# A GNN layer on one core: lead-in of the plan with longer transfers, bias parts from one row, message products by block, earlier due times

## The chip, the cores and the metric

The kernel runs on one core of a Trainium2 chip. The core has five engines that work side by side, each through its own queue in order: PE (TensorE, matmuls), DVE (VectorE), ACT (ScalarE), POOL (GpSimd) and SP (SyncE, which here only issues transfers). They wait for one another through semaphores. The metric is device time in microseconds; less is better. The time before is 669.11 us, the median of three runs.

## The reference

A graph with 6250 nodes of 128 features and 100,000 edges, sorted by their target. Each edge carries the source's features through one of two weight matrices, by the edge's type, and the messages are summed at the target. A third matrix is applied to the node itself; then come relu, the residual and a layer norm.

```
Xs = X[src]
m_data = Xs @ W_data.T + b_data
m_ctrl = Xs @ W_control.T + b_control
msg = jnp.where((edge_types == 0)[:, None], m_data, m_ctrl)
agg = jax.ops.segment_sum(msg, dst, num_segments=X.shape[0])
out = relu(agg + (X @ W_self.T + b_self))
x = _layernorm(x + out, axis=-1)
```

## The kernel before

**Messages.** There are 49 blocks of 128 nodes. For each block PE multiplies the node features (f32, from `xc`) with both message matrices in `w_sb` (L448) and adds the bias by a second matmul of a 0/1 matrix `one3` with `brows` (L450), whose first three rows hold the bias split into three bf16 parts that add up to the f32 value. Two blocks share a PSUM bank `g` of a ring of three. The sum is split into three bf16 parts as well and kept in SBUF as `m3`: for the first ten pairs (DQ) by ACT copies and DVE subtractions (L459 to L465, buffer `r1`), for the others by copies and matmuls with minus the identity (`minus`, L473). Each pair also goes to a table in memory (L479).

**Ranks.** Nodes are taken in 35 windows of 160 targets, in groups of 1, 2, and eight times 4 windows (GROUPS). For a group, `ranks` loads the windows' edges (`win`, 2688 edges each, 21 columns of 128), and for each of the 21 columns k it builds one-hot rows `hots` (L645, DVE), adds them up in the bank `rk` by matmuls with `tri` and `rest` (L655, PE) and takes the maximum (L659, DVE): the slot of each edge among the edges of its target window and source block. One column's reduce must be done before PE adds the next, so the 21 columns are a chain; `rk` and the `hots` exist once, so the groups follow one another as well. A packed map of slots is scattered (L674 to L689), written to memory (`packed`) and read back broadcast to all partitions as `rows`. Edges that found no slot are put in a list (L726 to L790, a row of short instructions), gathered from the table (`sr`) and joined as `gl`.

**Sums.** For each window and each of 25 quadruples of source blocks, stage 1 (L867) picks messages out of `m3` by `rows` into a `g` bank, ACT or DVE copies them to `gs` (L413 or L414), and stage 2 (L881, L884) adds them to the window's sums `a` by one-hot `hot` (L854). `close` then does relu, residual and layer norm. The last 650 nodes are summed another way: their edges' messages are gathered from the table tile by tile (`t_msg`, L931, L942).

**Where the edges of a window are** is found at the start: `r0` loads the target of every 200th edge (L257), DVE and PE count which lie below each window's first node, `er` gathers one row of 200 edges for each window (L353), and from it comes `first`, the first edge of each window (L375). Only group 0, which begins at edge 0, needs no `first`.

**What sets the order.** No engine's order is written out by hand. Each piece of work is given to a planner with its engine, an assumed length, a due time, what it reads and writes, and `lat`, the time from its end until its result can be used elsewhere. `Plan.run` then walks through a simulated time: on the engine that is free soonest it takes, among the work that is ready at that moment, that with the smallest due time. The program is issued in that order, and each engine keeps it on the chip, whatever the real lengths are. SP's transfers are assumed to take 0.1 us of the queue. Buffers of one name form a ring in the order of their first due time. Due times in the lead-in are:

- message products of pair q: 4 + 1.3 q
- ranks of group gi, column k: when + 2 + step k; the one-hot row 2 us sooner; the list at when + 6.5 + 21 step
- window w: from T0 + 13 w on, and the tiles of the last nodes from T0 + 2.5 x 13 on

**Lines that the prediction follows.** L257 `r0` load, L263 `b3` load, L335 to L351 counting, L353 `er`, L361 to L366 its use, L399 to L408 the bias parts on DVE, L439 `xc`, L448/L450 products, L502, L508, L511, L925 loads that `close` and the last nodes need (issued by SP at the start, as they wait for nothing), L606 to L659 ranks.

Of the kernel before, what the change touches and what calls it, by code (L numbers as in the profile page):

```python
# [23 lines left out]
D3 = 3 * D  # L24
# [206 lines left out]
def sums_over_windows(ctx, tc, x, xt, edges, w, bias, out, total):  # L231
# [16 lines left out]
    def C(shape, dtype, name):  # L248
        return Buf(plan, const, shape, dtype, name, 1)

    T0 = 46.0
    TW = 13.0
# [5 lines left out]
        r0.t, edges.rearrange("(p h k) c -> p h (k c)", p=125, h=RH)[:, :, 1:2]), 0.0, w=[r0],  # L258
        lat=2.0)
    w_sb = C([D, D3], F32, "w_sb")  # L260
    b3 = C([3, D3], F32, "b3")
    add("ACT", 0.1, lambda: A.dma_start(w_sb.t, w), 0.0, [], [w_sb], lat=2.5)
    add("ACT", 0.1, lambda: A.dma_start(b3.t, bias.to_broadcast([3, D3])), 0.0, [], [b3], lat=2.5)  # L263

# [77 lines left out]
    def count_rows():  # L342
# [13 lines left out]
        in_offset=bass.IndirectOffsetOnAxis(ap=row_i.t[:, 0:1], axis=0)),  # L356
        0.5, [row_i], [er], lat=2.5)
    dst_f = C([NBD, RL], F32, "dst_f")
# [19 lines left out]
    def load_edges(b, n, out_, due, buf, key, engine):  # L378
        def fn():
# [6 lines left out]
            else:  # L386
# [4 lines left out]

    part = C([3, D3], BF16, "part")
    left = C([3, D3], F32, "left")
    acc3 = C([3, D3], F32, "acc3")
    part2 = C([3, D3], BF16, "part2")
    brows = C([P, D3], BF16, "brows")
    bd = 2.0
    vec(1, D3, lambda: V.memset(brows.t, 0.0), [], [brows], 0.3)
    vec(bd, D3, lambda: V.tensor_copy(part.t, b3.t), [b3], [part])  # L399
    vec(bd, D3, lambda: V.tensor_scalar_mul(acc3.t, part.t, ident.t[:3, 0:1]),  # L400
        [part, ident], [acc3])
    vec(bd, D3, lambda: V.tensor_sub(left.t, b3.t, part.t), [b3, part], [left])
    vec(bd, D3, lambda: V.tensor_copy(part2.t, left.t), [left], [part2])
    vec(bd, D3, lambda: V.scalar_tensor_tensor(acc3.t, part2.t, ident.t[:3, 1:2], acc3.t,
                                               op0=ALU.mult, op1=ALU.add),
        [part2, ident, acc3], [acc3])
    vec(bd, D3, lambda: V.tensor_sub(left.t, left.t, part2.t), [part2, left], [left])
    vec(bd, D3, lambda: V.scalar_tensor_tensor(brows.t[:3, :], left.t, ident.t[:3, 2:3], acc3.t,  # L408
                                               op0=ALU.mult, op1=ALU.add),
        [left, ident, acc3], [brows])  # L410

# [18 lines left out]
    for q in range(NS):  # L430
# [12 lines left out]

        def products(bs=bs, c=c, xa=xa, mp=mp, q=q):
            for i, b in enumerate(bs):
                o = mp.t[:, 256 * i : 256 * i + 256]
                at = (b - c * CH) * P
                T.matmul(o, xa.t[:, at : at + P], w_sb.t[:, : 2 * D], start=i == 0, stop=False,  # L448
                         skip_group_check=True)
                T.matmul(o, one3.t, brows.t[:, : 2 * D], start=False, stop=q < DQ,  # L450
                         skip_group_check=True)
        add("PE", 0.55 * nb, products, due, [xa, w_sb, one3, brows], [mp])
        ts = slice(4 * q, 4 * q + 2 * nb)
# [499 lines left out]
    for gi, nw in enumerate(GROUPS):  # L953
        if gi == 0:
            when, step, engines = 4.0, 0.5, ["SP"]
        elif gi == 1:
            when, step, engines = 19.0, 0.9, ["SP", "ACT"]
        else:
            when, step, engines = T0 + w0 * TW - 58, 1.8, ["SP"]
            if gi == 2:  # L960
                when, step = 40.0, 1.3
        todo.append((gi, w0, nw, when, step, engines))
        w0 += nw
# [8 lines left out]
    total_tiles = sum(GT)  # L972
    g0, g1 = T0 + 2.5 * TW, T0 + (NW - 2.5) * TW
    done = 0
# [151 lines left out]
```

## Time and profile before

| | before |
|---|---|
| median of the runs | 669.11 us (669.08 to 672.03) |
| the profiled execution, its own time | 620.9 us |
| its span | 619.1 us |
| PE busy | 540.9 us (87%), 13418 matmuls |
| DVE busy | 521.1 us (84%) |
| ACT busy | 445.7 us (72%) |
| POOL busy | 115.1 us (19%) |
| mean granted TensorE clock | 0.982 |

The durations below come from that one profiled execution, whose time is 48.2 us less than the median of the timed runs. In a line of the timeline stand the start and length in microseconds, the engine, the line of the kernel, the operation, what it writes and reads, its shape, how often; and in brackets how long the engine stood idle just before and what ended that. A q behind an engine's name is its queue issuing a transfer. Names such as `brows` or `rk` are the program's own, with the numbers of buffers left out (so `one3` is "one", `b3` is "b").

### The profile page before, as it was taken

How to read it: one execution, taken by the hardware profiler on the slowest of the kernel's cores; microseconds unless marked ns; L12 is line 12 of the kernel's file. 1: busy time of each engine (PE TensorE's matmuls, PEld its weight loads, DVE VectorE, ACT ScalarE, POOL GpSimd, SP SyncE). 2: the span in 40 equal slices, each digit the busy share in tenths (PEclk: the TensorE clock that was granted, in tenths of full speed). 3: DMA queues.
4: the chain of work that ended last, by engine and by line, in shares of the span. 5: the costliest groups of instructions: out<-in, count | busy, mean ns of one | idle time of the engine just before them, and what ended most of it. 6: DMA issues, size and time to landing. Idle time of an engine off the chain costs nothing.

```text
span 619.1 us, 31669 instructions
## 1 busy us (share of the span) xinstructions
PE 540.9 (87%) x13418; PEld 415.5 (67%) x13418; DVE 521.1 (84%) x1846; ACT 445.7 (72%) x1153; POOL 115.1 (19%) x119
## 2 busy tenths in 40 slices
PE   3899959979998898989979998998899889998991
PEld 2555637757776677767767877777777678776670
DVE  4899789989999899988998999899988987866602
ACT  1477736757677767867867788778777777788991
POOL 1000230020421034310134410045100333110000
PEclk9999988989999999999999999999999999999997
DMA  4688651063135223540344143315420443043001
GB/s 113 194 269 266 196 178 38 25 207 104 44 103 153 84 65 100 177 127 5 118 141 140 51 134 99 101 50 168 133 85 4 156 122 109 24 139 105 27 4 28
DMA packets 58893, 67.85 MB, mean 110 GB/s; under 512 B 19707, under 2 KB 49906, under 8 KB 58743
## 3 DMA queue, kind: packets, MB, share of 16 engines
q1 hardware_dynamic: 45585, 48.25, 24.3%
q0 software_dynamic: 5664, 10.97, 6.7%
q10 hardware_dynamic: 7494, 6.53, 3.4%
q8 instruction: 107, 1.75, 1.1%
q14 instruction: 43, 0.35, 0.2%
HBM read 50.72 MB, written 13.27 MB: 103 GB/s over the span
## 4 chain that ended last, share of the span: by engine, by line
DVE 55%; PE 30%; ACT 5%; DMA 4%; issue 4%; SPq 1%; POOL 0%; ACTq 0%; DVEq 0%
DVE hot L854 10%; DVE slot L659 9%; PE a L881 9%; PE g L867 8%; DVE hots L645 4%; PE rk L655 4%; DVE rows L847 4%; DVE two L680 4%; ACT gs L413 3%; PE g L448 3%; DVE s L530 3%; DVE st L542 2%; DVE hr L674 2%; DVE xr L538 2%; PE a L884 2%
## 5 line engine op out<-in xcount | busy, mean ns | idle before, releaser
L413 ACT CAST gs<-g 128x384 bf16<-128x384 f32 x836 | 353.8, 481 | 93.5 <-PE g L867 88.6
L867 PE MATMUL g<-m,rows 128*32 128x384 bf16 x3430 | 316.8, 329 | 1.9 <-issue 1.1
L881 PE MATMUL a<-gs,hot 128*32 128x384 bf16 x3360 | 306.0, 331 | 9.1 <-ACT gs L413 5.1
L867 PEld LDWEIGHTS <-rows 128*32 128x32 bf16 x3430 | 217.4, 135 | 14.6 <-issue 2.1
L884 PE MATMUL a<-gs,hot 128*32 128x128 bf16 x2520 | 200.9, 220 | 0.1
L881 PEld LDWEIGHTS <-hot 128*32 128x32 bf16 x3500 | 153.4, 95 | 62.8 <-issue 27.0
L931 POOL DMA_INDIRECT t_msg<-table,t_idx x93 | 95.5, 1027 | 243.3 <-PE ga L942 196.9
L659 DVE TENSOR_REDUCE slot<-rk 128x4 f32<-128x392 f32 (+2 forms) x210 | 106.6, 507 | 18.2 <-PE rk L655 15.5
L854 DVE TENSOR_TENSOR hot<-iota_b,to_d 128x800 bf16<-128x800 bf16 x175 | 93.6, 565 | 21.0 <-PE a L884 16.6
L884 PEld LDWEIGHTS <-hot 128*32 128x32 bf16 x2625 | 98.0, 96 | 4.7 <-issue 0.3
L655 PE MATMUL rk<-hots,rest 128*32 128x392 bf16 (+2 forms) x800 | 73.2, 317 | 25.9 <-DVE slot L659 25.2
L655 PE MATMUL rk<-hots,tri 128*32 128x392 bf16 (+2 forms) x840 | 82.7, 314 | 0.0
L655 PEld LDWEIGHTS <-rest 128*32 128x32 bf16 x800 | 34.9, 96 | 48.4 <-issue 43.6
L645 DVE TENSOR_TENSOR hots<-iota_b,st 128x392 bf16<-128x392 bf16 (+2 forms) x210 | 60.1, 327 | 1.8 <-PE vt L689 1.6
L797 POOL DMA_INDIRECT sr<-table,at x18 | 17.1, 949 | 183.4 <-DVE at L785 99.9
L847 DVE TENSOR_SCALAR rows<-rows,pid 128x1568 bf16<-128x1568 bf16 x70 | 43.0, 635 | 0.0
L942 PE MATMUL ga<-t_msg,t_hot 128*32 128x384 bf16 x363 | 39.0, 326 | 2.7 <-DVE s L530 2.2
L655 PEld LDWEIGHTS <-tri 128*32 128x32 bf16 x840 | 36.3, 97 | 3.5 <-issue 0.3
L530 DVE TENSOR_TENSOR s<-s,a 128x128 f32<-128x128 f32 x70 | 19.8, 284 | 18.0 <-ACT s L527 16.8
L448 PE MATMUL g<-w_sb,xc 128*128 128x256 f32 x98 | 32.8, 430 | 1.3 <-PE rk L655 0.9
L689 PEld LDWEIGHTS <-two 128*64 128x64 bf16 x735 | 18.6, 108 | 16.7 <-DVE two L680 13.7
L689 PE MATMUL vt<-hots,two 128*64 128x98 bf16 x735 | 24.1, 208 | 6.0 <-DVE two L680 5.7
(174 smaller groups left out, 568.7 us busy)
## 6 DMA issues: line engine op xcount, KB each, us to landing
rows<-packed SPq DMA_DIRECT2D x35, 784.0 KB
table<-m SPq DMA_DIRECT2D x12, 384.0 KB
table<-m ACTq DMA_DIRECT2D x12, 384.0 KB
xc<-in_xt SPq DMA_DIRECT2D x8, 320.0 KB
xr<-in_x SPq DMA_DIRECT2D x8, 256.0 KB
out<-xr SPq DMA_DIRECT2D x8, 256.0 KB
gl<-sr SPq DMA_DIRECT2D x35, 48.0 KB
xc<-in_xt ACTq DMA_DIRECT2D x6, 256.0 KB
```

What stands on the lines that cost most here:

```text
L413: [("ACT", act(cols), lambda: A.copy(o(), src())), ("DVE", dve(cols), lambda: V.tensor_copy(o(), src()))], None, None, due, r, w, lat)
L448: T.matmul(o, xa.t[:, at : at + P], w_sb.t[:, : 2 * D], start=i == 0, stop=False, skip_group_check=True)
L645: vec(due - (2.0 if k else 0.5), nw * NT, lambda k=k, hot=hot, k0=k0: V.tensor_tensor(hot.t[:, k - k0].rearrange("p w (c d) -> p w c d", d=2),
L655: T.matmul(acc.t[R * j : R * j + R, : nw * NT], wt.t[:, R * j : R * j + R], m, start=start, stop=stop, skip_group_check=True)
L659: vec(due, nw * NT, lambda k=k: V.tensor_reduce(slot.t[:, k, :], acc.t[:, : nw * NT].rearrange("p (w c) -> p w c", c=NT), axis=AX.X, op=AL ...
L689: T.matmul(vv()[q : q + 64, i // 2, :], two.t[:, (k - k0) * nw + i].rearrange("p f r -> p (f r)"), hot.t[:, k - k0, i, :], start=k == 0 an ...
L847: add("DVE", dve(half * NT, 0.26), lambda sp=sp, rs=rs: V.tensor_scalar(sp.t[:, rs], sp.t[:, rs], pid1.t, None, op0=ALU.is_equal), due - 4 ...
L854: V.tensor_tensor(hot2.t[:, c0 : c0 + 5].rearrange("p g (c d) -> p g c d", d=2), iota1_b.t.rearrange("p (c d) -> p c d", d=2)[:, None].to_ ...
L867: T.matmul(gp.t[R * t : R * t + R, :D3], sp.t[:, :, 4 * g + t], m3.t[:, 4 * g + t, :], start=True, stop=True)
L881: T.matmul(a.t[R * j : R * j + R, :D3], hot2.t[:, g, R * j : R * j + R], gs.t, start=g == 0, stop=False, skip_group_check=True)
L884: T.matmul(a.t[R * c : R * c + R, D3:], hot2.t[:, g, P:], gs.t[:, c * D : (c + 1) * D], start=False, stop=last, skip_group_check=True)
L931: add("POOL", 1.25, lambda m=m, k=k: G.indirect_dma_start(out=m.t, out_offset=None, in_=table[:, :], in_offset=bass.IndirectOffsetOnAxis(a ...
```

## The change

Six edits, all in the part that runs ahead of window 3 or in the numbers that the planner goes by:

1. The base of the windows' due times, T0, goes from 46 to 36.
2. The planner's time from issue to use of the `r0` load goes from 2.0 to 4.5, that of the `er` gather from 2.5 to 6.5.
3. The bias is loaded as one row instead of three equal ones. Its three parts are made on one partition by two ACT copies and two DVE subtractions, and three transfers on SP put them in the three rows of `brows`. Seven DVE instructions on three partitions go.
4. The two blocks of a pair are given to the planner as two pieces of 0.58 instead of one of 1.1.
5. Ranks: group 0 starts at 3.0 instead of 4.0 with a step of 0.9 instead of 0.5; group 1 at 18.0 instead of 19.0 with 1.1 instead of 0.9; group 2 at 36.0 instead of 40.0 with the same 1.3. The groups from 3 on move with T0.
6. The tiles of the last nodes are spread from T0 + 2 x 13 to T0 + 33 x 13 instead of from T0 + 2.5 x 13 to T0 + 32.5 x 13.

```diff
-    T0 = 46.0
+    T0 = 36.0
...
-        lat=2.0)
+        lat=4.5)
     w_sb = C([D, D3], F32, "w_sb")
-    b3 = C([3, D3], F32, "b3")
+    b1 = C([1, D3], F32, "b1")
     add("ACT", 0.1, lambda: A.dma_start(w_sb.t, w), 0.0, [], [w_sb], lat=2.5)
-    add("ACT", 0.1, lambda: A.dma_start(b3.t, bias.to_broadcast([3, D3])), 0.0, [], [b3], lat=2.5)
+    add("ACT", 0.1, lambda: A.dma_start(b1.t, bias), 0.0, [], [b1], lat=2.5)
...
-        0.5, [row_i], [er], lat=2.5)
+        0.5, [row_i], [er], lat=6.5)
...
-    part = C([3, D3], BF16, "part")
-    left = C([3, D3], F32, "left")
-    acc3 = C([3, D3], F32, "acc3")
-    part2 = C([3, D3], BF16, "part2")
+    left = C([1, D3], F32, "left")
+    bparts = [C([1, D3], BF16, f"bpart{i}") for i in range(3)]
     brows = C([P, D3], BF16, "brows")
-    bd = 2.0
-    vec(1, D3, lambda: V.memset(brows.t, 0.0), [], [brows], 0.3)
-    vec(bd, D3, lambda: V.tensor_copy(part.t, b3.t), [b3], [part])
-    vec(bd, D3, lambda: V.tensor_scalar_mul(acc3.t, part.t, ident.t[:3, 0:1]),
-        [part, ident], [acc3])
-    vec(bd, D3, lambda: V.tensor_sub(left.t, b3.t, part.t), [b3, part], [left])
-    vec(bd, D3, lambda: V.tensor_copy(part2.t, left.t), [left], [part2])
-    vec(bd, D3, lambda: V.scalar_tensor_tensor(acc3.t, part2.t, ident.t[:3, 1:2], acc3.t,
-                                               op0=ALU.mult, op1=ALU.add),
-        [part2, ident, acc3], [acc3])
-    vec(bd, D3, lambda: V.tensor_sub(left.t, left.t, part2.t), [part2, left], [left])
-    vec(bd, D3, lambda: V.scalar_tensor_tensor(brows.t[:3, :], left.t, ident.t[:3, 2:3], acc3.t,
-                                               op0=ALU.mult, op1=ALU.add),
-        [left, ident, acc3], [brows])
+    vec(0.2, D3, lambda: V.memset(brows.t, 0.0), [], [brows], 0.3)
+    add("ACT", 0.4, lambda: A.copy(bparts[0].t, b1.t), 1, [b1], [bparts[0]])
+    vec(1, D3, lambda: V.tensor_sub(left.t, b1.t, bparts[0].t), [b1, bparts[0]], [left])
+    add("ACT", 0.4, lambda: A.copy(bparts[1].t, left.t), 1, [left], [bparts[1]])
+    vec(1, D3, lambda: V.tensor_sub(bparts[2].t, left.t, bparts[1].t), [left, bparts[1]],
+        [bparts[2]])
+    for i in range(3):
+        add("SP", 0.1, lambda i=i: S.dma_start(brows.t[i : i + 1, :], bparts[i].t), 1.5,
+            [bparts[i]], [(brows, i)], lat=2.0)
...
-        def products(bs=bs, c=c, xa=xa, mp=mp, q=q):
-            for i, b in enumerate(bs):
+        for i, b in enumerate(bs):
+            def product(i=i, b=b, c=c, xa=xa, mp=mp, q=q):
...
-        add("PE", 0.55 * nb, products, due, [xa, w_sb, one3, brows], [mp])
+            add("PE", 0.58, product, due, [xa, w_sb, one3, brows], [mp])
...
         if gi == 0:
-            when, step, engines = 4.0, 0.5, ["SP"]
+            when, step, engines = 3.0, 0.9, ["SP"]
         elif gi == 1:
-            when, step, engines = 19.0, 0.9, ["SP", "ACT"]
+            when, step, engines = 18.0, 1.1, ["SP", "ACT"]
         else:
             when, step, engines = T0 + w0 * TW - 58, 1.8, ["SP"]
             if gi == 2:
-                when, step = 40.0, 1.3
+                when, step = 36.0, 1.3
...
-    g0, g1 = T0 + 2.5 * TW, T0 + (NW - 2.5) * TW
+    g0, g1 = T0 + 2 * TW, T0 + (NW - 2) * TW
```

## The prediction

> **What bounds the kernel now.** I read the busy time by stretch first, cut where the windows start, then the order of time inside the stretches that stand out. Columns of the first: stretch, length, busy time of each engine (instructions), granted TensorE clock, DMA share, GB/s.
>
> ```profile
> 0.00:20.00 20.00, 9.12 (x36) 5.84 (x37) 11.73 (x60) 3.88 (x6) 2.59 (x8) 1.00 0.41 104
> 20.00:66.55 46.55, 42.80 (x460) 26.26 (x461) 42.28 (x198) 32.88 (x68) 0.00 (x0) 1.00 0.84 258
> 66.55:93.37 26.82, 19.74 (x488) 13.72 (x485) 21.28 (x83) 14.28 (x41) 9.45 (x10) 0.89 0.56 177
> 93.37:134.43 41.06, 35.84 (x861) 26.27 (x857) 38.77 (x131) 26.85 (x70) 4.84 (x5) 0.94 0.27 86
> 134.43:536.00 401.57, 369.15 (x9889) 294.65 (x9893) 367.40 (x1228) 305.18 (x802) 96.37 (x94) 1.00 0.33 101
> 536.00:619.10 83.10, 64.22 (x1703) 48.76 (x1695) 39.62 (x150) 62.60 (x169) 1.90 (x2) 0.94 0.18 57
> ```
>
> From 134.43 (window 3) to 536 PE and DVE are both 92% busy with the windows' even work, which the change doesn't touch. The slack lies ahead of window 3: PE idles 134.4 - 107.5 = 26.9 us there, DVE 134.4 - 114.1 = 20.3. Next, where in the lead-in:
>
> ```profile
> 8.37 1.85 SPq L511 DMA_DIRECT2D xb<-in_xt  x4
> 9.64 0.61 DVE L408 SCALAR_TENSOR_TENSOR brows<-left,ident,acc 3x384 bf16<-3x384 f32 x1
> 10.30 0.37 PE L450 MATMUL g<-brows,one 128*128 128x256 bf16 x1 [2.20 <-DVE brows L408]
> ...
> 11.22 0.43 SPq L502 DMA_DIRECT2D xrg<-in_x  x1
> ...
> 15.34 0.28 DVE L361 CAST dst_f<-er 41x200 f32<-41x200 int32 x1 [3.55 <-DMA er<-in_edges,row_i]
> ...
> 16.32 0.29 PE L370 MATMUL vt<-ident,first_f 41*1 41x41 f32 x2 [2.44 <-DVE first_f L366]
> ...
> 18.18 0.25 DVE L659 TENSOR_REDUCE slot<-rk 128x1 f32<-128x98 f32 x1
> ...
> 24.61 0.25 DVE L659 TENSOR_REDUCE slot<-rk 128x1 f32<-128x98 f32 x1
> ```
>
> DVE stands 3.55 us on the edge gather `er`, which the plan takes for landed, and everything behind it in DVE's order (r of L461 at 16.55) stands too; PE then waits 2.44 for `first_f`. So the first ranks step of group 0 ends only at 18.18 and the fifth at 24.61. Then the hole ahead of window 1:
>
> ```profile
> 81.24 0.36 DVE L659 TENSOR_REDUCE slot<-rk 128x2 f32<-128x196 f32 x1 [0.79 <-PE rk L655]
> ...
> 85.22 0.35 PE L655 MATMUL rk<-hots,rest 128*32 128x392 bf16 x4 [1.00 <-DVE slot L659]
> ...
> 89.51 0.52 PE L655 MATMUL rk<-hots,rest 128*32 128x392 bf16 x4 [1.71 <-DVE slot L659]
> ...
> 93.37 0.58 PEld L867 LDWEIGHTS <-rows 128*32 128x32 bf16 x12 [0.40 <-DVE rows L847]
> ```
>
> Window 0's last stage 1 is at 81.24, the same moment at which group 1's last ranks step ends; its list of spilled edges and the broadcast of its rows take 12.1 us more, and window 1 starts at 93.37. Ranks are one chain (one `rk` bank, one set of `hots`): group 0 (18.2 to 48.9), 1 (52.3 to 81.2), 2 (84.6 to 120.9). Window 3 needs group 2 and starts at 134.43, 6.0 after window 2's last stage 1 (128.4). **The lead-in is bound by the ranks chain, which PE and DVE share with the message products.**
>
> **What the skill says.** "Perfetto Trace Analysis", Optimization Strategy: regimes with another limit each are judged one by one; the table above agrees. "TensorE: Matmul & The Clock Gate", Architectural detail: DVE and ACT take their queue strictly in order; the 3.55 us at L361 agree. The same page, What's actually happening: after about 3.4 us idle the PE clock halves; in the 90-to-100 stretch of the trace the granted clock was 0.60. "DMA: Bandwidth & Descriptors", Anatomy of one DMA: about 2.0 us fixed for a transfer (fitted on the GpSimd path); here the small `r` load, issued from 1.29 for 1.00, was used at 5.65, so 3.3 us after its issue ended.
>
> **The change, part by part.**
>
> *Bias parts.* Seven DVE instructions go: .34+.40+.54+.35+.60+.54+.61 = 3.38 us. Two subtractions of 384 columns come (.54 each by the `left` row): 1.08. DVE net -2.3. Two ACT copies come, about .48 each (the 128x384 `gs` row); ACT is idle from 3.5 to 10.5, so nothing. Three row transfers to `brows` come on SP, .43 an issue. In the plan they are ready after about 3.4 us (b1 landed 2.8, copy, semaphore), when SP has already been given the 20 loads that need nothing (win, r, two xc, two and three xr, seven xb, two t_xc, two xrg: .1 each, 2.0 in all). On the chip those 20 take SP until 11.65. So the bias rows are issued from 11.65 to 12.95 and land 2.0 (the DMA page above, its fixed part) to 3.3 (`r`) later: 15.0 to 16.3; I take 15. The first product, L450 at 10.30 before, waits until then: **4.7 us later.** Nothing on SP waits behind them (its next issue was 18.30). This wait replaces the one on `er`.
>
> *Ranks sooner, lengths of transfers.* In the plan the bias rows are there at about 7.5 (2.8 for b1, four short ops and semaphores, 2.1 for the transfer), and the first `hots` at about 4.2. So the planner, which takes whatever is ready, puts some four ranks steps of group 0 ahead of the first product on PE: on the chip they run from 7 to 11, in time that PE idles anyway. With er at 6.5 instead of 2.5, `dst_f` goes in the plan to about 13.7, behind work that doesn't need it: the 3.55 on DVE and 2.44 on PE go; late next is the first product at 15. The r0 chain moves 1 to 2 us back behind the bias ops; it feeds the edges of group 1, loaded from 18.3 and used first at 37.1, so nothing.
>
> The count at 16.5: before, PE had done four blocks (4 x .54 at full clock) and no ranks step; after, four steps (.41 each) and one or two blocks at half clock. Same work, but the chain is ahead: fifth step at about 15 + 1.0 (one block at half clock) + .7 = 16.7 instead of 24.61, **8 us.** From there a step each 1.48 us as before (20.43, 21.91, 23.39: two blocks of .54 and a step of .41). The products are two blocks behind (1.1), hence the ranks gain and the products don't.
>
> *Products by block.* The same matmuls in two planned ops. A step's round (PE, semaphore, reduce, semaphore) was .9 when alone (23.72 to 24.61), longer than a block plus a step, shorter than two: it still waits for the second block. Worth 0 to .1 a step, below zero if the extra switches cost PE issue gaps (.32 each by the trace's "issue"); I take 0, ends -2 and +2.
>
> *T0 and dues.* Windows, gathers and groups from 3 on move together, so their order among themselves stays. Against the windows, group 1's list has 13 us less priority (due 44.4 against T0 46 before, 47.6 against 36 now), group 2's six less; the rows and hot2 of the next window gain it. I take 0 and keep -3 to +8.
>
> *The sum.* PE is 92% busy from 20 to 66.55, so window 0 stays at about 67 (five to six more ranks steps of .32 squeezed in, against the 1 us of clock and stalls gained). Group 1 ends at 73.5 instead of 81.24; plus 12.1 window 1 starts at 85.6, gain 7.8. Up to window 3 DVE is the limit: 114.1 - 2.3 = 111.8 busy; of its 20.3 idle I leave 15.5 (6.5 ahead of 20, where the bias wait stands; the rest as it was less the two holes): 127.3 against 134.4, **gain 7.1**. Afterwards the same work at the same rate. The profiled execution took 620.9 (span 619.1 and 1.8 around it): 613.8. The timed runs' median lies 48.2 higher, for a reason that the trace doesn't show; I carry the 7.1 over as it is: 669.11 - 7.1 = 662.0.
>
> **Rivals.**
> - *Forecast*, ranks chain earlier, DVE the limit: gain 4 to 11, 658 to 665. Chance .50.
> - *Both holes close.* The windows follow one another: 11.5 at window 1, 6 at window 3, some 2 of half clock: 19, so 650 (range 649 to 657). For: PE idles 26.9 there. Against: DVE would have to be busy 97% from the start. Chance .13.
> - *The bias rows eat it.* They land at 16.3 or later, the four early steps turn out to be one or two, and products and chain start together where they did: gain 0 +- 3, 669. Speaks for it: SP is full to 11.65 and PE, in order, can't pass the first L450. Chance .20.
> - *Slower: the list falls behind.* Group 1's list has 16 DVE instructions in a row (81.64 to 87.7). With due 47.6 it stands behind group 2's `hots` (36 + 1.3k) and reduces (38 + 1.3k) up to k = 7, before up to k = 1; one of them (.35 or .57) before each is 7 us, and group 2's list (69.8) now falls in the midst of window 2 (62 to 75) and waits likewise, 8 us. From a list of over 20 us instead of 12 it decides; with both, less the 8 of lead, +7: 676. Against: the list also paces the planner's own order, which gives it free DVE slots. Chance .17.
>
> **How the numbers follow.** 662 is the forecast's. The range, 650 to 674, takes in the second and third cases and the near half of the fourth. About .5% (3.3 us) can be told from no change: below 665.8 lie nearly all of the first two and a little of the third, .64; within, the rest of the third, .18; above 672.5, .18.
>
> **What would show it.** Right: the first L450 at 14 to 17 with its wait on a DMA of brows; four ranks reduces before it; no 3.5 us at L361; group 1's last reduce at 72 to 75, window 1 at 84 to 87, window 3 at 125 to 129, then 15 us a window. Wrong: the first L450 near 10 (the bias rows weren't late), window 1 at 82 (holes closed) or after 93 (list behind), or a rate after window 3 other than before.

## The result, and the profile after

| | before | changed |
|---|---|---|
| median, same chip, 15 runs each | 669.86 us | 673.85 us (671.58 to 676.02) |
| ratio | | 1.0052, 95% interval 1.0035 to 1.0070 |
| the profiled execution's span | 619.1 us | 671.3 us |

The change makes the kernel 0.5% slower; 1% faster was forecast. The two spans can't be set against each other, because the chips differ: on some the kernel before takes 624 us, on others 669, and the profile of before was taken on one of the first kind, that of the changed kernel on one of the second. I call them 624 chips and 669 chips, give every ratio against the kernel before on the same chip, and compare profiles within one kind. The changed kernel, run once more on a 624 chip (b0_after), gave 0.9984 (0.9968 to 1.0000), where I had expected 1.005.

First the busy time by stretch, cut where windows 0, 1, 3 and 31 start (columns: stretch, length, busy time of PE, PEld, DVE, ACT and POOL with instructions, clock, DMA share, GB/s). The profile after, on the 669 chip:

```profile
0.00:20.00 20.00, 5.12 (x44) 3.21 (x45) 9.40 (x65) 2.91 (x5) 2.77 (x8) 1.00 0.35 88
20.00:68.94 48.94, 47.08 (x452) 29.02 (x451) 42.35 (x184) 34.00 (x72) 0.00 (x0) 1.00 0.82 253
68.94:102.39 33.45, 22.66 (x483) 14.56 (x482) 21.46 (x89) 14.89 (x42) 9.57 (x10) 0.84 0.45 142
102.39:145.04 42.65, 35.01 (x865) 25.41 (x861) 39.06 (x132) 26.25 (x69) 6.73 (x6) 0.97 0.23 68
145.04:607.10 462.06, 408.40 (x10376) 308.59 (x10379) 384.46 (x1281) 325.43 (x845) 97.43 (x95) 0.99 0.31 94
```

The same program on a 624 chip (its span is 620.8):

```profile
0.00:20.00 20.00, 5.40 (x45) 3.35 (x46) 9.56 (x66) 3.02 (x5) 2.72 (x8) 1.00 0.35 88
20.00:69.20 49.20, 47.13 (x452) 28.91 (x451) 42.24 (x184) 33.86 (x71) 0.00 (x0) 1.00 0.81 252
69.20:95.30 26.10, 20.04 (x483) 13.85 (x486) 21.43 (x89) 14.65 (x42) 9.45 (x10) 0.87 0.59 180
95.30:136.10 40.80, 35.53 (x865) 25.76 (x861) 38.72 (x132) 26.37 (x69) 6.00 (x6) 0.92 0.27 82
136.10:556.40 420.30, 387.59 (x10375) 307.82 (x10379) 380.77 (x1281) 322.01 (x845) 99.11 (x95) 1.00 0.34 102
```

The lead-in is the same on both: window 0 starts at 68.94 and 69.20. The 50 us between the spans come afterwards, 42 of them in windows 3 to 31. By the medians the kernel before takes 45 us more on the 669 chip than on the 624 chip (669.86 against 624.67) and the changed kernel 51 (673.85 against 622.92). So most of the 50 goes with the chip, and some 6 with the chip and the change together.

On like chips the change does this. The kernel before has three profiles on 624 chips (the first, and the repeats a0_before and e0_before): window 0 starts at 66.6, 67.1 and 68.7, window 3 at 134.4, 135.0 and 135.8, and the spans are 619.1, 620.4 and 621.8. In the changed kernel PE has done 5.4 us of work by 20 where it had done 8.0 to 9.1. Window 0 comes at 69.2, and as 20 to 69.2 is 96% busy on PE, nothing is won back there. Window 3 comes at 136.1, 0.3 after the latest of the three, and the span of 620.8 lies among them. The forecast lead is absent on a 624 chip, and a loss can't be told there.

Where the first 20 us went, the changed kernel's timeline (the line numbers of these operations are 7 lower than in the kernel before: L443 is the bias product, L652 the ranks reduce, L402 the row transfers):

```profile
8.81 2.12 POOL L353 DMA_INDIRECT er<-in_edges,row_i  x1 [7.45 <-DVE hots L638]
9.61 0.25 DVE L652 TENSOR_REDUCE slot<-rk 128x1 f32<-128x98 f32 x1
...
12.11 1.90 SPq L402 DMA_DIRECT2D brows<-bpart  x3
...
18.02 0.40 PE L443 MATMUL g<-brows,one 128*128 128x256 bf16 x1 [7.56 <-DMA brows<-bpart]
...
23.44 0.23 PE L648 MATMUL rk<-hots,rest 128*32 128x98 bf16 x4
24.14 0.27 PE L443 MATMUL g<-brows,one 128*128 128x256 bf16 x1
24.68 0.27 PE L443 MATMUL g<-brows,one 128*128 128x256 bf16 x1
24.88 0.23 PE L648 MATMUL rk<-hots,tri 128*32 128x98 bf16 x4
25.37 0.25 DVE L652 TENSOR_REDUCE slot<-rk 128x1 f32<-128x98 f32 x1
...
26.81 0.29 DVE L361 CAST dst_f<-er 41x200 f32<-41x200 int32 x1
```

The waits on `er` (3.55 on DVE, 2.44 on PE) are gone: `dst_f` runs without one. Four ranks reduces end before 10, as forecast. But PE then stands 7.56 us at the first bias product, until 18.02, and six blocks go by before the second half of the fourth ranks step (`rest`, 23.44), two more before the first half of the fifth (`tri`, 24.88). So the fifth reduce comes at 25.37, later than the 24.61 of before.

Why 18.02, when the rows were issued by 14.01? The individual DMA records:

```
queue  record size  records      first start   last end
SP     48 B         15 of row 0  13.40         13.54
SP     48 B         15 of row 1  14.03         14.17
SP     48 B         15 of row 2  14.66         14.81
SP     48 B         3 (one each) 16.85         16.89
POOL   4800 B       20 (er)      11.65         16.51
```

Each row of 768 bytes is cut into 16 pieces of 48. Fifteen pieces land at once, and the sixteenth of all three rows only at 16.85; PE starts 1.1 us after the last of them. The records don't name their DMA engine, but their order points to it. From 15.28 to 16.53 one piece of 512 bytes of an earlier SP load runs between each two records of the `er` gather (4800 bytes, about 0.2 us each), without a gap; when the gather is through, nine more such pieces follow, and right behind them the last pieces of the rows. So the sixteenth pieces lay on the engine that carried the gather, behind pieces of SP's own earlier loads that came through one at a time. The Trainium skill, "DMA: Bandwidth & Descriptors", Queues, rings and completion order, says that a copy is split over up to 16 engines with a ring of its own on each, and that an engine takes turns between queues by whole packets; the records agree with the split and the turns, and show that a short piece can wait 2 to 3 us behind them.

### The profile page after: what moved, and what is told of

It reads as the page before. It is cut to its first block, busy times and chain, and to the rows that moved or that the text cites. A ratio compares the mean times of both kernels' runs of the same rounds, so it can differ in the third digit from the quotient of the medians.

```text
span 671.3 us, 31680 instructions
## 1 busy us (share of the span) xinstructions
PE 564.8 (84%) x13418; PEld 415.8 (62%) x13418; DVE 522.8 (78%) x1842; ACT 449.5 (67%) x1154; POOL 116.5 (17%) x119
## 4 chain that ended last, share of the span: by engine, by line
PE 50%; DVE 21%; ACT 9%; DMA 5%; issue 3%; another core or an unknown queue 2%; ACTq 0%; SPq 0%; DVEq 0%
PE a L874 17%; PE g L860 17%; ACT gs L406 7%; PE rk L648 6%; DVE hot L847 4%; DVE slot L652 4%; PE a L877 3%; PE ga L935 2%; DMA rows<-packed 2%; PE vt L682 2%; DVE two L673 2%; DVE s L523 2%; DVE rows L840 1%; DVE xr L531 1%
## 5 line engine op out<-in xcount | busy, mean ns | idle before, releaser
L860 PE MATMUL g<-m,rows 128*32 128x384 bf16 x3430 | 320.6, 330 | 6.7 <-issue 3.1
L652 DVE TENSOR_REDUCE slot<-rk 128x4 f32<-128x392 f32 (+2 forms) x210 | 107.0, 510 | 43.9 <-PE rk L648 17.3
L648 PE MATMUL rk<-hots,rest 128*32 128x392 bf16 (+2 forms) x800 | 74.7, 318 | 19.6 <-DVE slot L652 18.0
L648 PE MATMUL rk<-hots,tri 128*32 128x392 bf16 (+2 forms) x840 | 84.1, 317 | 6.6 <-DVE hots L638 5.8
L648 PEld LDWEIGHTS <-tri 128*32 128x32 bf16 x840 | 36.7, 98 | 10.6 <-DVE tri L312 5.1
L406 ACT CAST m<-g 128x512 bf16<-128x512 f32 (+1 forms) x43 | 23.0, 580 | 6.8 <-PE g L466 4.5
```

The source lines that it names most:

```text
L406: [("ACT", act(cols), lambda: A.copy(o(), src())), ("DVE", dve(cols), lambda: V.tensor_copy(o(), src()))], None, None, due, r, w, lat)
L648: T.matmul(acc.t[R * j : R * j + R, : nw * NT], wt.t[:, R * j : R * j + R], m, start=start, stop=stop, skip_group_check=True)
L652: vec(due, nw * NT, lambda k=k: V.tensor_reduce(slot.t[:, k, :], acc.t[:, : nw * NT].rearrange("p (w c) -> p w c", c=NT), axis=AX.X, op=AL ...
L860: T.matmul(gp.t[R * t : R * t + R, :D3], sp.t[:, :, 4 * g + t], m3.t[:, 4 * g + t, :], start=True, stop=True)
```

## Experiments

All ratios are to the kernel before on the same chip. PE busy is its busy time in the first 20 us of the profile; the other columns are the times at which the first bias product, the fifth ranks reduce of group 0, the last ranks reduce of group 1 and window 0 start. The a0_before run was made to find out why the two spans of the result differ; its span was expected at 666 to 670, or near 619 if the change itself had lost the 50 us. It came at 620.4 because its chip was a 624 chip, and b0_after shows that the second reading is wrong.

Two programs were timed on both kinds of chip: the changed kernel (0.9984 and 1.0052) and d1, which is e2 (0.9826 and 0.9866). Both come out 0.004 to 0.007 higher on the 669 kind. Even on one kind, a1 and e1 are one program and 0.0017 apart. So ratios of different kinds are not compared below by less than that.

| run | ratio (95%) | chip | PE busy by 20 | first bias product | fifth reduce | group 1's last reduce | window 0 |
|---|---|---|---|---|---|---|---|
| before (three profiles) | 1 | 624 | 8.0 to 9.1 | 10.3 to 10.5 | 24.6 to 26.8 | 81.2 to 82.8 | 66.6 to 68.7 |
| the changed kernel, in the result | 1.0052 (1.0035-1.0070) | 669 | 5.1 | 18.02 | 25.37 | 88.9 | 68.9 |
| a1_oldbias | 0.9915 (0.9885-0.9946) | 624 | 12.9 | 8.77 | 18.25 | 77.0 | 65.5 |
| a2_actrows | 0.9941 (0.9924-0.9958) | 624 | 7.9 | 15.09 | 21.51 | 77.4 | 64.7 |
| a3_olddues | 1.0010 (0.9993-1.0028) | 624 | 5.6 | 17.17 | 24.05 | 81.0 | 70.6 |
| b0_after (the changed kernel) | 0.9984 (0.9968-1.0000) | 624 | 5.4 | 17.75 | 25.33 | 81.8 | 69.2 |
| b1_biasonly | 0.9991 (0.9969-1.0013) | 624 | 6.2 | 16.68 | 25.19 | 81.9 | 67.4 |
| b3_ob_latold | 1.0032 (1.0016-1.0047) | 624 | 8.3 | 10.23 | 25.02 | 83.1 | 71.4 |
| c4_later | 0.9890 (0.9858-0.9923) | 624 | 12.7 | 10.28 | 17.16 | 74.6 | 62.0 |
| c7_rowlat11 | 1.0006 (0.9986-1.0025) | 669 | 5.8 | 22.33 | 10.46 | 84.8 | 70.5 |
| c6_later_lat5 | 0.9942 (0.9922-0.9962) | 669 | 10.6 | 13.64 | 10.52 | 81.4 | 64.3 |
| c1_ob_blkold | 0.9904 (0.9883-0.9926) | 669 | 12.9 | 8.77 | 18.62 | 81.6 | 60.6 |
| d1_ob_alldue | 0.9866 (0.9846-0.9886) | 669 | 13.5 | 8.20 | 19.30 | 82.8 | 64.4 |
| e1_oldbias (a1 again) | 0.9932 (0.9911-0.9953) | 624 | 12.7 | 8.82 | 17.32 | 74.1 | 62.7 |
| e2_ob_alldue (d1 again) | 0.9826 (0.9803-0.9850) | 624 | 13.5 | 8.16 | 19.41 | 76.7 | 64.4 |
| e3_later_olddue | 0.9898 (0.9873-0.9924) | 624 | 12.8 | 9.82 | 16.48 | 75.3 | 64.9 |
| f1_latonly | 0.9892 (0.9870-0.9913) | 669 | 13.3 | 8.21 | 19.18 | 82.7 | 60.3 |
| f2_ob_dueold | 1.0000 (0.9985-1.0015) | 669 | 13.6 | 8.07 | 19.28 | 85.6 | 64.9 |

### The bias rows and the queue that they stand in

**a1_oldbias: the changed kernel with the bias parts as before** (the DVE chain of before on three partitions, no row transfers).

> The kernel after, with only the bias parts made as before (three equal rows, seven DVE instructions, no row transfers). Theory A (the row transfers make the first product 8 us late, and that is the loss): first bias matmul near 10 us, 664 +- 3 us, ratio to before 0.987 to 0.996. Theory B (the lower due times put the lists and ranks behind the windows): 672 +- 2 us.

The first product comes at 8.77, the fifth reduce at 18.25, and the kernel is 0.9915 of before. So what is left of the change is worth 3 to 4 us more without its bias parts than with them (0.9915 here and 0.9932 in e1, against 0.9984 for the whole on the same kind of chip).

**a2_actrows: the row transfers issued by ACT instead of SP.**

```diff
-        add("SP", 0.1, lambda i=i: S.dma_start(brows.t[i : i + 1, :], bparts[i].t), 1.5,
+        add("ACT", 0.1, lambda i=i: A.dma_start(brows.t[i : i + 1, :], bparts[i].t), 1.5,
```

> The kernel after, with the three row transfers issued by ACT, which has nothing else to do there, instead of by SP behind 20 loads. Theory A by the queue alone: rows landed by 10 us, ahead of the edge gather, first bias matmul near 10 us instead of 18, 663 +- 3 us. If the wait is for the DMA engine that carries the gather and not for the queue: no change, 673. Theory B: 672 +- 2 us.

The timeline of this kernel on ACT (ACTq is its queue issuing a transfer), and what DVE and PE wait for:

```profile
3.74 0.51 ACT L396 CAST bpart<-b 1x384 bf16<-1x384 f32 x1
...
9.98 0.63 ACTq L402 DMA_DIRECT2D brows<-bpart  x1
10.65 0.51 ACT L398 CAST bpart<-left 1x384 bf16<-1x384 f32 x1 [6.41 <-DMA t_xc<-in_xt]
11.19 1.16 ACTq L402 DMA_DIRECT2D brows<-bpart  x2
11.20 0.55 DVE L399 TENSOR_TENSOR bpart<-left,bpart 1x384 bf16<-1x384 f32 x1 [4.99 <-ACT bpart L398]
...
12.24 0.72 PE L344 MATMUL vt<-ones,begun 125*41 125x1 f32 x8 [5.62 <-DVE begun L337]
...
15.09 0.42 PE L443 MATMUL g<-brows,one 128*128 128x256 bf16 x1
```

The first part is there at 4.25, but its row is issued only at 9.98, and ACT's next copy shows 6.41 us of idle time, which the profile puts down to the landing of `t_xc`, one of SP's loads. Why ACT's issue waited for that, no run here tells. It holds up more than the rows: DVE stands 4.99 us for ACT's second copy, PE 5.62 us for `begun`, which comes behind it in DVE's order, and the first bias product at 15.09 stands behind that work and shows no wait of its own. So this run is no clean test of SP's queue. The product is 2.7 us sooner than in the changed kernel, and part of the gain is there (0.9941).

**c4_later: the sixteen loads that feed only later work (`xr`, `xb`, `t_xc`, `xrg`) are given `brows` as something that they read, so the planner puts them behind the row transfers on SP.**

```diff
-        ... xr.t[:m0, :nw, :], pick(x)), due - 20, [],
+        ... xr.t[:m0, :nw, :], pick(x)), due - 20, [brows],
```

(and likewise for the other three).

> The kernel after, with the 16 loads that close and the last nodes need given to SP behind the three row transfers instead of ahead of them. Theory A1 (SP's queue makes the rows late): rows issued by 7.5 us, landed ahead of the edge gather, first bias matmul at 9 to 11, fifth ranks step at 16 to 19, window 3 at 128 to 131, ratio 0.983 to 0.991, better than with the old bias parts (0.9915). Theory A2 (the rows wait for what lies on the DMA engines, whoever issues them): first bias matmul stays at 15 or later, ratio 0.994 to 1.005.

The timeline of this kernel, and its first 20 us by engine:

```profile
4.55 2.92 SPq L402 DMA_DIRECT2D brows<-bpart  x3
...
10.28 0.42 PE L443 MATMUL g<-brows,one 128*128 128x256 bf16 x1
...
17.16 0.25 DVE L652 TENSOR_REDUCE slot<-rk 128x1 f32<-128x98 f32 x1
```

```profile
0.00:20.00 20.00, 12.65 (x91) 8.22 (x91) 15.39 (x79) 7.86 (x14) 2.72 (x8) 1.00 0.44 117
```

The rows are issued at 4.55 instead of 12.11, the bias product at 10.28 shows no wait, PE has 12.65 us of work done by 20, and the kernel is 617.34 us where the changed kernel on the same chip takes 622.92. So 5.6 us of what the change earns is lost to the place of three transfers in SP's queue. That is shown; the share that the turns behind `er` have in it isn't told apart, since the rows here are ahead of `er` too.

**b1_biasonly: the kernel before with the new bias parts alone.**

> The kernel before, with the new bias parts alone. Theory A: first bias matmul at 16 to 19, the wait on the edge gather lies within that of the rows and is not paid again, ratio 1.004 to 1.012. If the bias parts alone cost nothing (0.997 to 1.002), the loss comes from the rows together with the longer transfer times in the plan.

This alone gives 0.9991, no difference, although the first product goes from 10.3 to 16.68. Its timeline says why:

```profile
15.15 0.29 DVE L361 CAST dst_f<-er 41x200 f32<-41x200 int32 x1 [3.80 <-DMA er<-in_edges,row_i]
...
16.68 0.39 PE L443 MATMUL g<-brows,one 128*128 128x256 bf16 x1 [4.01 <-DMA brows<-bpart]
```

With the old lengths in the plan DVE stands on `er` until 15.15 in any case. The two waits lie side by side, and the second costs nothing that this run can tell while the first is there.

### The longer lengths of r0 and er

**b3_ob_latold: the changed kernel with the bias parts and these two lengths as before**, and **f1_latonly: the kernel before with these two lengths changed and nothing else.**

```diff
-        lat=2.0)
+        lat=4.5)
...
-        0.5, [row_i], [er], lat=2.5)
+        0.5, [row_i], [er], lat=6.5)
```

> The kernel after with the old bias parts and also the old, short transfer times in the plan; due times and blocks as after. If the 0.85% that the kernel with the old bias parts gains comes from DVE and PE no longer standing on the edge gather, it goes: DVE stands over 3 us on it again, fifth ranks step at 23 to 25, ratio 0.997 to 1.001. If it comes from the due times or the blocks: 0.990 to 0.994.

> The kernel before with two numbers changed: the plan counts the transfers of r0 at 4.5 instead of 2.0 and of er at 6.5 instead of 2.5. If these lengths are the whole gain of the kernel with old bias parts and old due times (0.9866 and 0.9826), 0.981 to 0.989 here, with the cast of er at 18 to 19 without its long wait and the fifth reduce at 18 to 20. If the products by block are needed for it, 0.992 to 1.0.

Without them, the rest of the change (due times, products by block) is 1.0032, slower than before; they alone are 0.9892, or 7.3 us of 670.05. The timeline of f1 and its first 20 us:

```profile
8.21 0.42 PE L450 MATMUL g<-brows,one 128*128 128x256 bf16 x1
...
18.33 0.28 DVE L361 CAST dst_f<-er 41x200 f32<-41x200 int32 x1
...
19.18 0.24 DVE L659 TENSOR_REDUCE slot<-rk 128x1 f32<-128x98 f32 x1
```

```profile
0.00:20.00 20.00, 13.32 (x92) 8.74 (x92) 16.92 (x72) 8.19 (x14) 2.24 (x8) 1.00 0.64 185
```

DVE doesn't stand on `er` any more, the reduces come 5.4 us sooner, and PE has 13.3 us of work done by 20 instead of about 9. This is the gain that the change holds, and two numbers carry it; which of the two counts was not tried.

### How far ahead the ranks chain is worth having

**c7_rowlat11: the plan counts the row transfers at 11.0 instead of 2.0**, which is about when they land; **c6_later_lat5: c4_later with 5.0.**

```diff
-            [bparts[i]], [(brows, i)], lat=2.0)
+            [bparts[i]], [(brows, i)], lat=11.0)
```

> The changed kernel with one number other: the plan counts each of the three row transfers at 11.0 instead of 2.0, so that it takes the rows for landed at about 16.5 instead of 7.5. The transfers themselves and SP's order ahead of them stay, so the rows must still land at 17 to 18 on the chip. Theory A (the lead of the ranks chain was lost because the plan, taking the rows for early, put six product blocks ahead of the fifth ranks step, and the real wait for the rows then held the chain too): ten ranks steps or so run ahead of the first product, the fifth reduce ends by 12 instead of 25.3, group 1 ends some 5 earlier than in the changed kernel, and the kernel is 0.985 to 0.993 of before. Theory B (the late products themselves cost the time, whatever stands ahead of them): the chain's lead is given back by products and numerators that come late for window 0, window 0 starts at 69 or later, and the time is that of the changed kernel, 0.998 to 1.003.

> The changed kernel with the sixteen loads of the later chunks (xr, xb, t_xc, xrg) planned behind the row transfers, as in the earlier experiment that gave 0.989, and the row transfers counted at 5.0 instead of 2.0 in the plan. First bias product at 10 to 11 as there. Theory A (the chain's lead counts): the plan puts five or six ranks steps ahead of the first product instead of four, the fifth reduce ends by 12 (17.2 there), and the time is 0.984 to 0.989 of before. Theory B (lead beyond what products allow is worth nothing): the same as there within 0.3%, 0.987 to 0.992.

Reduces and first product of c7, and its first 20 us:

```profile
10.46 0.25 DVE L652 TENSOR_REDUCE slot<-rk 128x1 f32<-128x98 f32 x1
...
15.00 0.26 DVE L652 TENSOR_REDUCE slot<-rk 128x1 f32<-128x98 f32 x1 [0.46 <-PE rk L648]
...
15.71 0.26 DVE L652 TENSOR_REDUCE slot<-rk 128x1 f32<-128x98 f32 x1 [0.46 <-PE rk L648]
16.03 0.27 PE L648 MATMUL rk<-hots,rest 128*32 128x98 bf16 x4 [0.36 <-DVE slot L652]
...
21.44 0.26 DVE L652 TENSOR_REDUCE slot<-rk 128x1 f32<-128x98 f32 x1 [1.33 <-PE rk L648]
22.33 0.42 PE L443 MATMUL g<-brows,one 128*128 128x256 bf16 x1
...
38.92 0.25 DVE L652 TENSOR_REDUCE slot<-rk 128x1 f32<-128x98 f32 x1
```

```profile
0.00:20.00 20.00, 5.76 (x119) 3.22 (x119) 13.94 (x92) 2.83 (x6) 2.72 (x8) 1.00 0.35 89
```

Thirteen reduces are through by 20, where the kernel before had one. Still c7 is 1.0006, within theory B's range. Against the changed kernel on the same kind of chip (1.0052) that is 0.5% faster, so the lead is worth something, but less than theory A had it. Alone the chain goes at 0.71 us a step, and both engines wait in each (0.36 on PE, 0.46 on DVE): PE has 5.76 us of work done by 20, hardly more than in the changed kernel. And the lead doesn't last. After the fifteenth step, at 21.44, no step runs until 38.92: the sixteenth is due at 18.5 (3.0 + 2 + 0.9 x 15), behind twelve pairs of products that are due from 4.0 to 18.3, and 25 product blocks go through PE in that gap. The 15 us of lead at the fifth step are 4 at group 1's last reduce (84.8 against 88.9). So this run doesn't show what a chain would be worth that stays ahead.

c6 gains less than both of its theories had, 0.9942: its fifth reduce came at 10.52, as theory A had it, but the first product only at 13.64, where both had 10 to 11. Whether it is slower than c4 (0.9890) isn't told, as c4 ran on a 624 chip and c6 on a 669 chip.

### Due times and products by block

**a3_olddues: the changed kernel with all due times as before; c1_ob_blkold: with bias parts and pair products as before; d1_ob_alldue: with bias parts and all due times as before** (the due times are T0, the spread of the last nodes' tiles, and groups 0 to 2, parts 1, 5 and 6 of the diff).

> The kernel after, with T0, the spread of the last nodes' tiles and the due times of groups 0 to 2 as before; bias parts, transfer lengths and blocks as after. Theory A: 674 +- 2 us, first bias matmul still at 18 us. Theory B: 664 +- 3 us, window 1 at 95 us or sooner.

> The changed kernel with the bias parts and the pair of message products per planned step as before (only the longer transfers in the plan and the new due times are left). Against the same kernel with products by block (0.9915 of before): if the split is worth nothing, as the prediction has it, 0.989 to 0.994; if the split lets ranks steps in between two blocks, the chain is slower here and the time 0.996 to 1.001.

> The changed kernel with the bias parts and all due times (window start, gathers, groups 0 to 2) as before; left are the longer transfers in the plan and the products by block. Against the kernel with the new due times and old bias parts (0.9915): if the longer lengths of er and r0 carry the gain, 0.990 to 0.996 here; if the earlier due times carry it, 0.998 to 1.003.

Beside the late rows the new due times gain little or nothing (1.0010 without, 0.9984 with, on two 624 chips, and the intervals overlap). c1 is at 0.9904, within the expectation for a split that is worth nothing; but the same with blocks (0.9915 and 0.9932) was timed on 624 chips only and c1 on a 669 chip, so beside the new due times the split isn't judged by it. But d1 is at 0.9866, better than its two theories: with the bias early, the old due times looked like the better ones. The next four runs were made for that.

**e1_oldbias and e2_ob_alldue** (a1 and d1 again, on one chip), **e3_later_olddue** (c4 with all due times as before), **e0_before** (the kernel before, profiled beside them).

> The kernel before once more, for its profile on the chip of the three runs beside it; nothing is changed. If this chip is one of those on which the profiled run of the changed kernel took some 50 longer, waits of DVE and ACT that no recorded event ends (remote) of several microseconds must stand in this profile too, right after the first windows begin, and windows 3 to 31 must take about 460 instead of 421; if they are absent here, they belong to the change and not to the chip.

> The changed kernel with the bias parts as before (new due times, longer transfers in the plan, products by block), which gave 0.9915 on another chip. Beside the same with old due times, on the same chip. If the new due times are worth the 1.6 microseconds that they gave beside the new bias rows: 0.985 to 0.988 if the other stays at 0.9866. If with early bias rows the old due times are the better ones: 0.989 to 0.994.

> The changed kernel with the bias parts and all due times as before, which gave 0.9866 on another chip. If the difference of 0.5% to the same with new due times came from the due times, it repeats on this chip, at least 0.25% below the kernel beside it; if it came from the chips, both are within 0.2% of each other.

> The changed kernel with the sixteen later loads planned behind the row transfers (0.989 before) and all due times as before. If the old due times are the better ones wherever the bias rows are early: 0.983 to 0.987, the best of all. If not: 0.988 to 0.993.

On one chip e1 is 620.60 us and e2 614.34: the difference repeats, and with the old bias parts the new due times cost 6.3 us. With the new bias parts issued early they cost nothing that can be told (e3 0.9898, c4 0.9890); the hoped-for sum didn't come. On one chip e3 is 3.5 us slower than e2 (617.80 against 614.34), so beside the old due times the new bias parts cost time even when they are early. e0's chip was a 624 chip, so its profile (span 621.8) could not say what the kernel before does on a 669 chip, and that stays open.

**f2_ob_dueold: as e1, but with the due times of groups 0 to 2 as before too**, so that of the due times only T0 and the spread of the last tiles are new. It ran beside f1.

> The changed kernel with the bias parts and the due times of groups 0 to 2 as before, the window start and gathers at the new due times. If the due times of the groups cost the 1% by which the kernel with all new due times was slower, 0.982 to 0.988 here; if the earlier window start costs it, 0.991 to 0.995, and windows 31 to 34 take about 39 to 40 as with the new times instead of 37.5.

It gives 1.0000 beside the 0.9892 of f1 on the same chip, 7.8 us more; the two differ in T0, the spread and the products by block. d1, on another 669 chip (0.9866), differs from f1 in the blocks alone and is no slower, and from f2 in T0 and the spread alone. So beside products by block and the groups' old due times, the earlier T0 with its spread costs 8 to 9 us. That is not its price everywhere: c1 has the new T0 and spread too, with the groups' new due times and the products by pair, and at 0.9904 on a 669 chip it can't be told from f1. Whether the groups' due times or the pairs spare it the cost stays open; e1, with the groups' new due times and with blocks, still loses 6.3 us to e2, on a 624 chip. One piece of the cost can be seen in the last windows. From the start of window 31 to that of window 34 in e1 (new due times), then in e2 (old ones):

```profile
548.50:588.70 40.20, 35.21 (x887) 26.85 (x887) 20.61 (x71) 33.38 (x91) 0.00 (x0) 0.96 0.16 54
```

```profile
551.60:589.20 37.60, 33.25 (x886) 25.47 (x881) 20.19 (x71) 33.10 (x91) 0.00 (x0) 1.00 0.16 58
```

The same matmuls take 2.6 us longer with the new T0, with the granted clock at 0.96 instead of 1.00. In every profile with the new T0 and spread this stretch is 38.8 or 40.1 to 40.2 long, in every one with the old ones it is 37.4 to 37.7. The 1.4 us between 38.8 and 40.2 don't come with the program alone: a1 is the same program as e1 and has 38.8, at a clock of 1.00. In e1 one wait stands there, in the timeline:

```profile
557.18 0.51 PE L881 MATMUL a<-gs,hot 128*32 128x384 bf16 x4 [2.16 <-DVE gs L414]
```

and in the stretch 556 to 560 the clock was 0.65. f2 and f1 show the same (40.10 against 37.40). Their spans are 10.5 us apart (669.5 and 659.1): 3.0 of it is there when window 3 starts, 4.8 comes in windows 3 to 31 and 2.8 in this stretch. In e1 and e2 the remaining 4 to 5 us aren't located: the profiled executions have spans of 614.2 and 614.7, while their medians are 6.3 apart.

## Why the prediction was wrong

**What bounds the lead-in: not refuted.** I called the ranks chain the bound, and one column of the table goes with that: group 1's last reduce parts the runs on both kinds of chip. On 624 chips it stands at 74.1 to 77.4 in the runs with 0.983 to 0.994 and at 81.0 to 83.1 in those with 0.998 to 1.003; on 669 chips at 81.4 to 82.8 (0.987 to 0.994) and at 84.8 to 88.9 (1.000 to 1.005). PE's work by 20 parts them less well: it is about 13 us in most of the faster runs, but f2 has 13.6 and is at 1.000, and a2 has 7.9 and is at 0.994. A column that goes with the time is not yet its cause; no run moved the end of the chain and nothing else. But c4, where the fifth step came at 17.16 (16.7 forecast), bears out the rest of the forecast's sum: group 1's last reduce 74.6 (73.5), window 1 at 87.9 (85.6), window 3 at 129.1 (127.3), and 7.3 us gained (7.1; 617.34 against 624.67). What failed in the change as it was made is the step that puts the chain ahead.

**Bias rows: the mechanism right, the size wrong.** The prediction had twenty loads ahead of them on SP, issue from 11.65 to 12.95, and took landing at 15; the issue was 12.11 to 14.01 (0.63 each, not 0.43), and they were used at 18.02. The page's fixed 2.0 us was the value I chose and 3.3 my upper end; 4.0 was measured from the last issue's end. The piece behind `er` is what neither end of the bound had in it. The rival that put the landing at 16.3 or later was right in this.

**The wait on `er`: right.** Both waits went, and f1 prices the two lengths at 7.3 us. That this is close to the forecast 7.1 is luck: 7.1 was the sum for the whole change, from a fifth step 8 us sooner and rows that were late, and in f1 the fifth step is 5.4 us sooner and no rows are sent. In the changed kernel the first product was due late next, as the prediction said, and was later than it said.

**The fifth step at 16.7: this is the step that failed.** The prediction put "about 15 + 1.0 (one block at half clock) + .7". Four steps did run early, but one block was the wrong count: once the plan has the rows (at 7.5), the first three pairs are due at 4.0, 5.3 and 6.6 and the fourth step (3.0 + 2 + 0.9 x 3) at 7.7, so six blocks go to PE ahead of its second half, and the next pair (7.9) ahead of the fifth step (8.6). The chip keeps that order: the chain waits for the rows and then for eight blocks, from 18.02 to 24.88. Of the 8.7 us between 16.7 and 25.37, 3.0 are the rows (18.02 instead of 15) and 5.7 the blocks and the step behind them (7.35 instead of 1.7). The lead of "8 us" was one of -0.8. In c4, with the first product at 10.28, the chain went behind the blocks too, and the fifth step came 6.9 us after it. The due times in the front of this document were enough to see it; I looked at which work was ready and not at which was due first.

**What followed from it fell too** (624 chip): group 1's last reduce 81.8, 73.5 forecast; window 1 at 95.3, 85.6 forecast; window 3 at 136.1, 127.3 forecast. "The bias rows eat it" ("products and chain start together where they did: gain 0 +- 3") is the rival that came, though four steps ran early and not one or two: by the medians -1.8 us on the 624 chip (622.92 against 624.67), which lies in it, and +4.0 on the 669 chip, 1 us beyond.

**The list falls behind: not what happened.** Its sign "window 1 after 93" is there, but from group 1's last reduce to window 1 it is 13.5 us on either chip, against 12.1 before and the "over 20" from which that rival decides.

**Due times at 0, kept from -3 to +8** (plus is slower): about -1.6 beside the late rows, not told from nothing, and +6.3 beside the old bias parts. "Afterwards the same work at the same rate" was wrong for the last windows: 38.8 us from window 31 to window 34 in the changed kernel on the 624 chip, 37.4 before.

**Products by block at 0 (-2 to +2):** with old due times nothing told apart (f1 and d1); with new ones not tried on one kind of chip. **DVE net -2.3:** its busy time went from 521.1 to 518.7 on the 624 chip. The cost of the `r0` chain was not tried by itself.

**Why +4.0 on one chip and -1.8 on the other** is not settled. On the 669 chip the profile after has stalls that no recorded event ends, the first of them just where group 1's last steps and the first gathers of the last nodes meet:

```profile
79.68 0.94 POOL L924 DMA_INDIRECT t_msg<-table,t_idx  x1 [0.30 <-issue]
81.14 0.36 DVE L652 TENSOR_REDUCE slot<-rk 128x2 f32<-128x196 f32 x1 [6.15 <-remote]
81.55 0.36 PE L648 MATMUL rk<-hots,rest 128*32 128x196 bf16 x4 [2.18 <-DVE slot L652]
81.99 0.48 ACT L406 CAST gs<-g 128x384 bf16<-128x384 f32 x1 [4.66 <-remote]
```

DVE stands 6.15 us and ACT 4.66 with no event that ends it, and PE's next ranks matmul waits for DVE. All seven profiles on 669 chips have such waits of over 2 us (c7, c6 and d1: 4.9, 3.3 and 3.7 between 60 and 100), and none of the thirteen on 624 chips has one, of the same program or another. So they go with the chip, but what they cost the kernel before was never profiled.

## What to carry to other kernels

When a transfer is put on a queue, count what the queue will really have issued ahead of it: the plan charged SP 0.1 us an issue, the chip took 0.4 to 0.6, and three rows behind twenty loads came 10 us later than planned; moving the loads behind them gained 5.6 us. Where a plan's transfer lengths were too short, setting them right was the gain (two numbers, 0.989; with products by block 0.983 to 0.987, the best of the runs and better than both kernels). And a serial chain that is ahead at its start need not be ahead at its end: c7's stood still for 17 us as soon as its due times came behind those of other work, and alone it leaves both its engines waiting. So follow the chain to the step that the next work needs, in the order that the due times give, before its lead is counted.

## What was not expected of the hardware

Transfers of 768 bytes waited 2 to 3 us for one sixteenth of themselves, which by the order of the records lay behind twenty records of another queue's gather: 15 pieces of 48 bytes of each row were there by 14.81 and the last ones at 16.89. And one program took 620.8 us on one chip and 671.3 on another, with the same granted clock of about 0.98 and the same times up to 70 us. Stalls of up to 6 us on DVE and ACT that no recorded event ends are part of the difference, and in windows 3 to 31 PE's busy time for the same matmuls is 408.4 us instead of 387.6, at a clock of 0.99 instead of 1.00; the cause of both stays open.
